# Adding b2 - beta1 on GpSimd instead of by a product with ones, in a four-layer graph kernel on one core

## The chip, the cores and the metric

The kernel runs on one core of one Trainium2 chip. The metric is the device time of one execution in microseconds (us), lower is better. In the profile PE is TensorE (PEld its weight loads), DVE is VectorE, ACT is ScalarE, POOL is GpSimd and SP the engine that issues most of the DMAs.

## What is computed

The input is x, 64 graphs of 256 nodes with 256 features, and adj, a 256 x 256 adjacency matrix for each. Four layers follow each other, each x = layernorm(x + layer(x, adj)) over the features. All is float32.

```python
# layer 0: 4 heads of 64
attn = softmax(where(adj == 0, -1e9, q @ k.T / 8));  out = (attn @ v) @ Wo.T + bo;  out = norm(out) * gamma + beta
# layer 1: 8 heads of 32, one projection for q, k and v, then an MLP
n = norm(x) * gamma1 + beta1
x = x + attention(n, n, n, adj)
y = norm(x) * gamma2 + beta2
out = x + gelu(y @ W1 + b1) @ W2 + b2
# layer 2: graph attention, leaky_relu(s1 + s2) as scores;  layer 3: edge scores by adj == 1..4
```

## The kernel before, in words

`usual_input` does the work; `any_input` is a slower second way that is taken when a flag says that the values are unusual, and is not taken here. A group is two graphs, so 512 rows in four blocks of 128; there are 32 groups. `group(g)` is a generator: each `yield` ends a *turn*, and a group has 45 turns. Several groups are in work at the same time, each in another stage, and the row `ORDER` says in which order their turns are written into the program: in period p the digit a stands for the next turn of group p - a. `FIRST` and `LAST` do the same for the ramps. `prepare`, the setup that the first groups do not need at once, is one more generator and takes its turns beside group 0.

The order of PE is exactly the order in which its instructions are written: `matmul` and `transpose` chain them. On the other engines a scheduler places the instructions of all groups in the queue, so an instruction of a later turn can stand ahead of one of an earlier turn.

The turns of a group that the text speaks of (L numbers are lines of the kernel before):

| turns | what they do |
|---|---|
| 1 to 3 | loads of x and adj; adj to bfloat16 (adjb, L889) and its square sum (L890) on ACT; four transposing DMAs to adjT (L897) |
| 4 | mask on DVE (L900, adjT and adjb); transposes of x on PE, copies on ACT (L584) |
| 5 to 7 | q, k and v projections; then x + beta0 on POOL (L717), which waits for the transposes of x |
| 8 to 10 | layer 0: scores, exp on ACT (L605), times mask on DVE (L607), products with v and with ones; reciprocal of the sums (L641) |
| 11 to 13 | sums over DRAM to all rows (lines, rr); oT times rr on DVE (L732); product with Wo |
| 14, 15 | two norms on DVE with the power of the variance on POOL (L547, L551); the results are z (L559) and xb (L750) |
| 17 | transposes of z on PE, to zT (L586, ACT) |
| 18 to 22 | layer 1: four times scores of 16 matmuls on 32 rows, exp (L605), times mask on DVE with sums (L613, 8 for each), products with z |
| 21, 23, 24 | in `behind`: transposes back, x2 = y / sums + xb (L770, L773), `both` = x2 + xb on POOL (L774), norm to xb (L559) |
| 26 to 30 | transposes of xb, W1 and gelu on ACT (L788) |
| 31 to 34 | W2, a graph in two turns of 8 float32 products each, 16 records of the profile |
| 33, 35 | y = W2 product + `both` on DVE (L699), norm to xn |
| 36 to 40 | layer 2 |
| 41 to 45 | layer 3; the result goes out by DMA |

The second product of the MLP needs x2 + xb - beta1 + b2 added, since xb carries beta1. Before the change POOL makes x2 + xb, and b2 - beta1 comes in on PE: `b2m` holds it in three rows of bfloat16, whose sum is the float32 value nearly to the last bit, and `onesb` has ones in three rows and zeros elsewhere. A product of the two, 128 x 128 by 128 x 512 in bfloat16, opens each accumulation (`row` in `project`). In PSUM there are two score tiles (`ps`, two banks each) and four tiles of one bank (`pm`).

Of the kernel before, what the change touches and what calls it, by code (L numbers as in the profile page):

```python
# [8 lines left out]
F32 = mybir.dt.float32  # L9
BF16 = mybir.dt.bfloat16  # L10
# [3 lines left out]
ALU = mybir.AluOpType  # L14
AX = mybir.AxisListType

P = 128
N = 256
D = 256
NC = D // P  # L20
G = 2
QB = N // P
# [11 lines left out]
AT_ONCE = 3  # L34


ORDER = "011225334342343542234235432323132121321132121"


FIRST = "0010000201000100213100110101000000100"  # L40
# [360 lines left out]
def usual_input(ctx: ExitStack, tc: tile.TileContext, a: dict, out: bass.AP, flag: bass.AP):  # L401
# [7 lines left out]
    nc = tc.nc  # L409
    B = a["x"].shape[0]  # L410

    const = ctx.enter_context(tc.tile_pool(name="const", bufs=1))
# [44 lines left out]
    def load_rows(name, cols, queue=None):  # L457

        src = a[name]
        t = const.tile([P, src.shape[0] // P, cols], F32, name=name)  # L460
        load(queue, t, src.rearrange("(c p) f -> p c f", p=P))
        return t
# [7 lines left out]
    setup = act.tile([P, NF, T], F32, name="setup", tag="hT", bufs=1).rearrange("p f t -> p (f t)")  # L470

    def load_all(src, name, at=None):

        t = const.tile([P, D], F32, name=name) if at is None else setup[:, at:at + D]
        load(None, t, src.unsqueeze(0).to_broadcast([P, D]))
        return t
# [18 lines left out]
    beta1r = load_all(a["L1_gnn_beta1"], "beta1r")  # L495
    gamma1r = load_all(a["L1_gnn_gamma1"], "gamma1r", 256)
    b2 = load_all(a["L1_gnn_b2"], "b2", 512)
# [7 lines left out]
    w2 = load_rows("L1_gnn_W2", D)  # L505

    wa1 = const.tile([P, 2, NC], F32, name="wa1")
    b2m = const.tile([P, D], BF16, name="b2m")
    onesb = const.tile([P, P], BF16, name="onesb")
    bop = const.tile([P, D], F32, name="bop")  # L510
    bounds = const.tile([P, 2], F32, name="bounds")

# [1 line left out]
    def over_blocks(v, n=TB):  # L514
        return v.unsqueeze(1).to_broadcast([P, n, D])
# [3 lines left out]
    def in_order(ins):  # L519

        if on_pe:
            tc.add_manual_dep(ins.ins, on_pe.pop(),
                              mybir.DependencyInfo(mybir.DependencyClass.NoSync, mybir.DependencyReason.DATA),
                              reason="the order of the program")
        on_pe.append(ins.ins.name)

    def matmul(*args, **kw):
        in_order(nc.tensor.matmul(*args, **kw))  # L528

    def transpose(*args):  # L530
        in_order(nc.tensor.transpose(*args))  # L531

    def blocks(i):
        return range(i * QB, (i + 1) * QB)
# [22 lines left out]
    def scaled(dst, src, i, mv, rstd):  # L557
        for q, t in enumerate(blocks(i)):
            nc.vector.tensor_scalar(dst[:, t, 0:D], src[:, t, 0:D], mv[:, q, 0:1], rstd[:, q:q + 1],  # L559
                                    ALU.subtract, ALU.mult)  # L560

    ALL = range(G)
# [114 lines left out]
            go_on()  # L677
            yield

    def project(dst, srcT, w, extra, row=None, gs=ALL):  # L680


        chunks = w.shape[1]
        for i in gs:
            pm = ps_m.tile([P, QB, D], F32, name="pm")
            if row is not None:
                matmul(pm, onesb, row.unsqueeze(1).to_broadcast([P, QB, D]), start=True, stop=False)
            for q in range(QB):
                t = i * QB + q
                for c in range(chunks):  # L690
                    matmul(pm[:, q, :], srcT[:, c, t * P:(t + 1) * P], w[:, c, :],
                           start=c == 0 and row is None, stop=c == chunks - 1 and (row is None or q == QB - 1))
                if chunks > NC:
                    yield
            o = dst[:, i * QB:(i + 1) * QB, :]
            if extra is None:
                nc.scalar.copy(o, pm)
            else:
                nc.vector.tensor_tensor(o, pm, extra[:, i * QB:(i + 1) * QB, 0:D], ALU.add)  # L699
# [56 lines left out]
    def layer1(xb, z, mask):  # L756

        zT = transposed(z, gamma1, beta1)
        x2 = act.tile([P, TB, D], F32, name="y")
        both = act.tile([P, TB, W], F32, name="both", tag="xn")  # L760
        yield

        def behind(i, oT, r):
            nc.vector.reciprocal(r, r)
            pt = ps_m.tile([P, QB, D], F32, name="pm")
            for q in range(QB):
                for c in range(NC):
                    transpose(pt[:, q, c * P:(c + 1) * P], oT[:, c, q * P:(q + 1) * P], ident)
            o = x2[:, i * QB:(i + 1) * QB, :]
            nc.vector.tensor_tensor(o.rearrange("p q (h d) -> p (q h) d", d=32), pt.rearrange("p q (h d) -> p (q h) d", d=32),  # L770
                                    r.rearrange("p q c h -> p (q c h)").unsqueeze(2).to_broadcast([P, QB * 8, 32]), ALU.mult)
            xi = xb[:, i * QB:(i + 1) * QB, :]
            nc.vector.tensor_tensor(o, o, xi, ALU.add)  # L773
            nc.gpsimd.tensor_tensor(both[:, i * QB:(i + 1) * QB, 0:D], o, xi, ALU.add)  # L774
            yield
            mv, rstd = stats(x2, i)
            scaled(xb, x2, i, mv, rstd[:, 0])
            yield

        yield from attention(zT, zT, z, mask, 32, gamma1, behind)  # L780
        yT = transposed(xb, gamma2, beta2)
        yield
        hT = act.tile([P, NF, T], F32, name="hT", bufs=1)
        for f in range(NF):
            pm = ps_m.tile([P, T], F32, name="pm")
            for c in range(NC):
                matmul(pm, w1[:, c, f * P:(f + 1) * P], yT[:, c, :], start=c == 0, stop=c == NC - 1)
            nc.scalar.activation(hT[:, f, :], pm, AF.Gelu, bias=b1[:, f:f + 1])  # L788
            if f % 2:
                yield  # L790
        return x2, hT, both
# [93 lines left out]
    def group(g):  # L885
        x, adj = load_group(g) if g else first
        yield
        adjb = io.tile([P, TB, N], BF16, name="adjb", bufs=1)
        nc.scalar.activation(adjb, adj, AF.Copy, accum_out=there[:, g:g + 1])  # L889
        nc.scalar.activation(adj.bitcast(F32), adj, AF.Square, bias=minus_half, accum_out=edges[:, g:g + 1])  # L890
        yield


        pt = io.tile([P, G, QB, N], BF16, name="adjT", bufs=1)
        for t in range(TB):
            i, q = divmod(t, QB)
            nc.sync.dma_start_transpose(pt[:, i, :, q * P:(q + 1) * P], adjb[:, t, :])  # L897
        yield
        mask = act.tile([P, G, QB * N], BF16, name="mask")
        nc.vector.scalar_tensor_tensor(mask.rearrange("p g k -> p (g k)"), pt.rearrange("p g k q -> p (g k q)"), 1.0,  # L900
                                       adjb.rearrange("p t k -> p (t k)"), ALU.mult, ALU.min,
                                       accum_out=both_ways[:, g:g + 1])
        xb, z = yield from layer0(g, x, mask)
        y, hT, both = yield from layer1(xb, z, mask)

        def others(gs):

            yield from project(y, hT, w2, both, b2m, gs)
            x = yield from renormed(y, gs)
            x = yield from layer2(x, mask, gs)  # L910
            x = yield from layer3(g, x, mask, gs)
            i, j = g * G + gs[0], g * G + gs[-1] + 1
            nc.sync.dma_start(out[i:j].rearrange("b (q p) d -> p (b q) d", p=P), x[:, gs[0] * QB:(gs[-1] + 1) * QB, 0:D])

        if g < B // G - 1:
            yield from others(ALL)
            return

        parts = [others((i,)) for i in ALL]
        turn = 0  # L920
        while parts:
            for r in parts[:turn // QB + 1]:
                if next(r, END) == END:
                    parts.remove(r)
            turn += 1
            yield

    def prepare():
# [8 lines left out]
        pm = ps_m.tile([P, D], F32, name="pm")  # L937
# [12 lines left out]

        yield

        nc.gpsimd.memset(onesb, 0.0)
        nc.gpsimd.memset(onesb[0:3, :], 1.0)
        nc.gpsimd.memset(b2m, 0.0)
        left = setup[:, 2304:2560]
        nc.vector.tensor_tensor(left, b2, beta1r, ALU.subtract)
        for k in range(3):
            part = setup[:, 3328 + k * P:3456 + k * P].bitcast(BF16)
            nc.vector.tensor_copy(part, left)  # L960
            nc.sync.dma_start(b2m[k:k + 1, :], part[0:1, :])
            if k < 2:
                nc.vector.tensor_tensor(left, left, part, ALU.subtract)

        yield

        sq = setup[:, 2816:3328].rearrange("p (s d) -> p s d", s=2)
        nc.vector.tensor_tensor(sq[:, 0], gamma1r, gamma1r, ALU.mult)
# [8 lines left out]
        pm = ps_m.tile([P, 2], F32, name="pm")  # L977
# [26 lines left out]
    for period in range(len(groups)):  # L1004
        for age in ORDER:
            g = period - int(age)
# [22 lines left out]
    pm = ps_m.tile([P, 1], F32, name="pm")  # L1029
# [38 lines left out]
```

## The time and the profile before

| | us |
|---|---|
| median of the three runs shown | 2663.03 |
| lowest, highest | 2661.43, 2664.4 |
| span of the profiled execution | 2658.2 |
| PE busy | 2586.9 (97%) |
| DVE, ACT, POOL busy | 1965.7, 1293.9, 592.3 |
| b2m products on PE (64) | 24.6 in all by their own length, 384 ns each |
| adds of `both` on POOL (64) | 81.4, 1272 ns each |
| adds of beta0 on POOL (32) | 77.7, 2430 ns each |

The profiled execution has no time of its own beside its span; the median of the runs is 4.8 us above that span, for what lies before the first and after the last instruction. In a group of instructions of the profile, "busy" counts overlapping lengths once; matmuls are pipelined, so what one costs PE is read from its start to the start of the next.

### The profile page before, as it was taken

Reading aid. Unit: us, or ns where it says so; the run is one execution under the profiler, and the core shown is the slowest. Engines: PE = TensorE matmul, PEld = TensorE weight load, DVE = VectorE, ACT = ScalarE, POOL = GpSimd, SP = SyncE. Lnnn points to the kernel's source line nnn. Section 1 sums busy time; section 2 is a strip of 40 time slices with the busy share of each in tenths; the row PEclk is TensorE's granted clock in tenths of the full one; section 3 lists DMA queues with packets and bytes.
Section 4 is the critical chain, followed back from the end, with each engine's and each line's share of the span. In section 5 each row is a group of like instructions: output and inputs, shape, how many; then the busy total and the mean of one; then the engine's idle time right before and its main releaser. Section 6 shows DMA issues by size and latency. Waiting matters only on the chain.

```text
span 2658.2 us, 44921 instructions
## 1 busy us (share of the span) xinstructions
PE 2586.9 (97%) x16648; PEld 1761.5 (66%) x16648; DVE 1965.7 (74%) x6189; ACT 1293.9 (49%) x1997; POOL 592.3 (22%) x1145
## 2 busy tenths in 40 slices
PE   6899999999999999999999999999999999999996
PEld 3567667666667666666676666676676676676665
DVE  4667777777777777777777777777777777777774
ACT  3445544545545545545455544555445455445442
POOL 2112222222222222222222222222222222222121
PEclk8999999999999999999999999999999999999998
DMA  6001011001010000010010110110110101000000
GB/s 163 25 9 32 26 37 37 25 29 29 29 37 29 33 29 28 29 37 27 28 36 25 33 37 25 29 37 21 36 37 25 29 29 29 29 21 17 17 1 25
DMA packets 113393, 83.20 MB, mean 31 GB/s; under 512 B 44304, under 2 KB 112656, under 8 KB 113168
## 3 DMA queue, kind: packets, MB, share of 16 engines
q1 hardware_dynamic: 111552, 78.94, 10.1%
q8 instruction: 134, 2.20, 0.4%
q10 hardware_dynamic: 1360, 0.79, 0.1%
q0 software_dynamic: 256, 0.53, 0.1%
q14 instruction: 91, 0.75, 0.1%
HBM read 54.80 MB, written 17.04 MB: 27 GB/s over the span
## 4 chain that ended last, share of the span: by engine, by line
PE 71%; DVE 17%; POOL 9%; issue 2%; DMA 1%; ACT 0%; SPq 0%; DVEq 0%; POOLq 0%; ACTq 0%
PE pm L528 55%; PE ps L528 10%; PE pm L531 7%; POOL rstd L551 6%; DVE st L544 3%; DVE y L816 2%; DVE y L744 2%; DVE xn L559 2%; POOL ve L547 2%; DVE z L559 2%; DVE mv L545 1%; DVE xb L750 1%; DVE y L743 1%; DVE r L815 1%; POOL ve L549 0%
## 5 line engine op out<-in xcount | busy, mean ns | idle before, releaser
L613 DVE SCALAR_TENSOR_TENSOR e<-e,mask 128x256 f32<-128x256 f32 x1024 | 428.2, 483 | 130.7 <-ACT e L605 130.7
L605 ACT ACTIVATE e<-ps 128x1024 f32<-128x1024 f32 x384 | 371.9, 1020 | 196.2 <-PE ps L528 176.3
L528 PE MATMUL pm<-L_gnn_W,hT 128*128 128x256 f32 x2048 | 463.0, 379 | 0.0
L528 PE MATMUL pm<-xT,L_gnn_W 128*128 128x512 f32 x1024 | 455.2, 592 | 0.0
L528 PEld LDWEIGHTS pm<-L_gnn_W,hT 128*128 128x128 f32 x2048 | 384.5, 190 | 49.2 <-issue 0.7
L788 ACT ACTIVATE hT<-pm,b 128x512 f32<-128x512 f32 x256 | 176.7, 691 | 408.1 <-PE pm L528 408.0
L528 PEld LDWEIGHTS pm<-xT,L_gnn_W 128*128 128x128 f32 x1024 | 191.7, 190 | 203.4 <-issue 198.5
L544 DVE BATCH_NORM_STATS2 st<-y 128x6 f32<-128x256 f32 x768 | 301.1, 408 | 6.7
L551 POOL TENSOR_TENSOR rstd<-ve,mhalf 128x2 f32<-128x2 f32 (+1 forms) x384 | 298.4, 777 | 26.7
L559 DVE TENSOR_SCALAR xn<-y,mv,rstd 128x256 f32<-128x256 f32 x384 | 141.9, 411 | 178.9 <-POOL rstd L551 178.8
L547 POOL TENSOR_SCALAR ve<-mv 128x2 f32<-128x2 f32 x384 | 98.9, 257 | 741.0 <-DVE mv L545 738.8
L774 POOL TENSOR_TENSOR both<-y,xb 128x512 f32<-128x512 f32 x64 | 81.4, 1272 | 764.2 <-DVE y L773 764.2
L607 DVE TENSOR_TENSOR e<-e,mask 128x1024 f32<-128x1024 f32 x128 | 150.8, 1221 | 15.3 <-ACT e L605 15.3
L528 PE MATMUL ps<-xT 32*128 32x256 f32 x2048 | 148.0, 402 | 2.2 <-ACT e L605 1.3
L586 ACT ACTIVATE xT<-pm,beta,gamma 128x512 f32<-128x512 f32 x128 | 92.3, 770 | 104.4 <-PE pm L531 104.3
L528 PE MATMUL pm<-e,z 128*32 128x256 f32 x2048 | 142.4, 387 | 0.3
L528 PEld LDWEIGHTS ps<-xT 32*128 32x128 f32 x2048 | 93.2, 185 | 74.0 <-issue 66.8
L528 PE MATMUL pm<-e,v 128*32 128x256 f32 x2048 | 125.4, 384 | 8.0 <-DVE e L607 8.0
L528 PE MATMUL pm<-L_gnn_WoT,oT 128*128 128x256 f32 x512 | 121.2, 391 | 8.3 <-DVE oT L732 6.0
L528 PE MATMUL ps<-qT,kT 64*128 64x256 f32 x1024 | 128.0, 389 | 0.5 <-ACT e L605 0.5
L528 PE MATMUL pm<-xT,L_gnn_WqT 128*128 128x512 f32 x256 | 120.9, 616 | 3.7 <-ACT xT L584 3.7
L816 DVE SCALAR_TENSOR_TENSOR y<-pm,r,xn 128x256 f32<-128x256 f32 x256 | 120.9, 473 | 2.5
(138 smaller groups left out, 4059.1 us busy)
## 6 DMA issues: line engine op xcount, KB each, us to landing
x<-in_x SPq DMA_DIRECT2D x32, 512.0 KB
adj<-in_adj SPq DMA_DIRECT2D x32, 512.0 KB
rr<-lines SPq DMA_DIRECT2D x124, 128.0 KB
out<-xn SPq DMA_DIRECT2D x31, 512.0 KB
adjT<-adjb SPq DMA_TRANSPOSE x128
L_gnn_W<-in_L_gnn_W SPq DMA_DIRECT2D x2, 1024.0 KB
lines<-zs SPq DMA_DIRECT2D x62, 4.0 KB
rr<-lines POOLq DMA_DIRECT2D x4, 128.0 KB, 3.3
```

What stands on the lines that cost most here:

```text
L528: in_order(nc.tensor.matmul(*args, **kw))
L531: in_order(nc.tensor.transpose(*args))
L544: nc.vector.bn_stats(st[:, q, :], src[:, t, 0:D])
L547: nc.gpsimd.tensor_scalar(ve[:, 0], mv[:, :, 1], EPS, None, ALU.add)
L551: nc.gpsimd.tensor_tensor(rstd, ve, mhalf[:, 0:k * QB].rearrange("p (k t) -> p k t", k=k), ALU.pow)
L559: nc.vector.tensor_scalar(dst[:, t, 0:D], src[:, t, 0:D], mv[:, q, 0:1], rstd[:, q:q + 1], ALU.subtract, ALU.mult)
L586: nc.scalar.activation(dst[:, c, on], pt[:, on], AF.Identity, bias=bias[:, c:c + 1], scale=scale[:, c:c + 1])
L605: nc.scalar.activation(e, ps, AF.Exp, scale=scale)
L607: nc.vector.tensor_tensor(e, e, mask.unsqueeze(1).to_broadcast([P, 2, QB * N]), ALU.mult)
L613: nc.vector.scalar_tensor_tensor(e[:, h, k], e[:, h, k], 1.0, mask[:, k], ALU.mult, ALU.mult, accum_out=sums[:, kc, c, j:j + 1])
L788: nc.scalar.activation(hT[:, f, :], pm, AF.Gelu, bias=b1[:, f:f + 1])
L816: nc.vector.scalar_tensor_tensor(y[:, t, :], po[:, 0:D], r, x[:, t, 0:D], ALU.mult, ALU.add)
```

## The change

Two things change. First, b2m becomes a float32 tile with b2 - beta1 in all 128 rows, made by one subtraction in `prepare`; the three bfloat16 parts, their three DMAs, `onesb`, three memsets and one turn of `prepare` go. `project` loses the product that opened the accumulation, and a second POOL operation in `behind`, written after the norm to xb, adds b2m to `both`. Second, ORDER is another row with the same number of digits of each kind.

```diff
-ORDER = "011225334342343542234235432323132121321132121"
+ORDER = "510324231342354343452223431232321232111321213"
...
-    b2m = const.tile([P, D], BF16, name="b2m")
-    onesb = const.tile([P, P], BF16, name="onesb")
+    b2m = const.tile([P, D], F32, name="b2m")
...
-    def project(dst, srcT, w, extra, row=None, gs=ALL):
+    def project(dst, srcT, w, extra, gs=ALL):
...
-            if row is not None:
-                matmul(pm, onesb, row.unsqueeze(1).to_broadcast([P, QB, D]), start=True, stop=False)
...
                     matmul(pm[:, q, :], srcT[:, c, t * P:(t + 1) * P], w[:, c, :],
-                           start=c == 0 and row is None, stop=c == chunks - 1 and (row is None or q == QB - 1))
+                           start=c == 0, stop=c == chunks - 1)
...
             xi = xb[:, i * QB:(i + 1) * QB, :]
+            bi = both[:, i * QB:(i + 1) * QB, 0:D]
             nc.vector.tensor_tensor(o, o, xi, ALU.add)
-            nc.gpsimd.tensor_tensor(both[:, i * QB:(i + 1) * QB, 0:D], o, xi, ALU.add)
+            nc.gpsimd.tensor_tensor(bi, o, xi, ALU.add)
             yield
             mv, rstd = stats(x2, i)
             scaled(xb, x2, i, mv, rstd[:, 0])
+            nc.gpsimd.tensor_tensor(bi, bi, over_blocks(b2m, QB), ALU.add)
             yield
...
-            yield from project(y, hT, w2, both, b2m, gs)
+            yield from project(y, hT, w2, both, gs)
...
-        nc.gpsimd.memset(onesb, 0.0)
-        nc.gpsimd.memset(onesb[0:3, :], 1.0)
-        nc.gpsimd.memset(b2m, 0.0)
-        left = setup[:, 2304:2560]
-        nc.vector.tensor_tensor(left, b2, beta1r, ALU.subtract)
-        for k in range(3):
-            part = setup[:, 3328 + k * P:3456 + k * P].bitcast(BF16)
-            nc.vector.tensor_copy(part, left)
-            nc.sync.dma_start(b2m[k:k + 1, :], part[0:1, :])
-            if k < 2:
-                nc.vector.tensor_tensor(left, left, part, ALU.subtract)
-
-        yield
+        nc.vector.tensor_tensor(b2m, b2, beta1r, ALU.subtract)
```

With the turns of the table, the two rows read as follows from the place where the first W2 turn (31) stands; the number in brackets is the age of the group.

```
before: 31(3) 17(2) 32(3) 18(2) 33(3)  4(1) 34(3) 19(2)  5(1) 20(2)  6(1) 35(3) 21(2)  7(1)  8(1) 36(3) 22(2)  9(1) 23(2) 10(1)
after:  31(3)  4(1) 17(2) 32(3) 18(2) 33(3) 19(2)  5(1) 20(2) 34(3) 21(2)  6(1)  7(1)  8(1) 35(3) 22(2)  9(1) 23(2) 10(1) 36(3)
```

## The prediction

> **What bounds the kernel now.** I read the page's head first: which engine is full, and which chain ended last.
>
> ```profile
> span 2658.2 us, 44921 instructions
> PE 2586.9 (97%) x16648; PEld 1761.5 (66%) x16648; DVE 1965.7 (74%) x6189; ACT 1293.9 (49%) x1997; POOL 592.3 (22%) x1145
> PE 71%; DVE 17%; POOL 9%; issue 2%; DMA 1%; ACT 0%; SPq 0%; DVEq 0%; POOLq 0%; ACTq 0%
> ```
>
> TensorE (PE) is the bound, and its order is written by hand. So a product that is taken away pays in full, and any late input of PE costs in full. The add of beta0 (POOL L717) starts at 1023.43 and again at 1103.90, 1184.23: one period of ORDER is 80.33 us. Here is PE in the part that the new row rearranges (columns: start, duration, engine, line, operation; idle before in brackets).
>
> ```profile
> 1089.14 0.38 PE L528 MATMUL pm<-b2m,onesb 128*128 128x512 bf16 x1
> 1089.35 3.62 PE L528 MATMUL pm<-L_gnn_W,hT 128*128 128x256 f32 x16
> 1092.81 0.38 PE L531 MATMUL pm<-ident,z 128*128 128x128 f32 x2
> 1093.48 1.16 PE L531 MATMUL pm<-ident,z 128*128 128x128 f32 x6 [0.29 <-DVE z L559]
> 1094.48 3.62 PE L528 MATMUL pm<-L_gnn_W,hT 128*128 128x256 f32 x16
> 1098.03 1.15 PE L528 MATMUL ps<-xT 32*128 32x256 f32 x16
> 1099.11 0.39 PE L528 MATMUL pm<-b2m,onesb 128*128 128x512 bf16 x1
> 1099.33 3.62 PE L528 MATMUL pm<-L_gnn_W,hT 128*128 128x256 f32 x16
> 1102.79 1.04 PE L531 MATMUL pm<-ident,x 128*128 128x128 f32 x8
> 1103.66 3.62 PE L528 MATMUL pm<-L_gnn_W,hT 128*128 128x256 f32 x16
> 1107.21 1.15 PE L528 MATMUL ps<-xT 32*128 32x256 f32 x16
> ```
>
> Read start to start, since matmuls are pipelined. The bias product takes 0.21 us (1089.14 to 1089.35). The eight transposes of z take 1.67 us (1092.81 to 1094.48) where the same eight of x take 0.87 (1102.79 to 1103.66): PE loses 0.80 us there, waiting for VectorE's z. The first scores of layer 1 (1098.03) come 9.18 us before the second (1107.21). From 1000 to 2400 us the list of PE's waits has this one line (total, times, longest; it counts less than start to start, as ends are modelled):
>
> ```profile
> PE pm L531 <- DVE z L559: 5.3, 18, 0.3
> ```
>
> Then the other engines in the same stretch, from their timelines:
>
> ```profile
> 1093.74 0.88 DVE L750 SCALAR_TENSOR_TENSOR xb<-z,rstd,beta1r 128x256 f32<-128x256 f32 x2
> 1096.58 1.23 DVE L900 SCALAR_TENSOR_TENSOR mask<-adjT,adjb 128x1024 bf16<-128x1024 bf16 x1
> 1104.04 2.57 DVE L613 SCALAR_TENSOR_TENSOR e<-e,mask 128x256 f32<-128x256 f32 x1
> ```
> ```profile
> 1103.90 2.43 POOL L717 TENSOR_TENSOR x<-x,beta 128x1024 f32<-128x1024 f32 x1 [2.97 <-PE pm L531]
> ```
> ```profile
> 1097.84 1.06 ACT L889 ACTIVATE adjb<-adj 128x1024 bf16<-128x1024 int32 x1 [2.15 <-DVE mask L900]
> 1100.17 1.92 ACT L605 ACTIVATE e<-ps 128x1024 f32<-128x1024 f32 x2
> ```
>
> Two things are to be seen. An L613 takes 0.42 us, but the one under GpSimd's L717 takes 2.57: 2.15 us longer. The steady periods all show it. And ScalarE's queue holds the exponentials of layer 1 (L605) behind adjb (L889), which waits for VectorE's mask (L900).
>
> [...] bn_stats under GpSimd's L774 keep their length (0.75 us for two at 1125.13, 0.75 at 1098.86 without). [...]
>
> **The change, part by part.** I use the trace's durations and the order of the two built programs, on this period's clock.
>
> 1. *Bias product gone.* 64 x 0.21 = 13.4 us of PE, all on the path: 0.43 per period with two, and 6 outside the 29 steady periods with the new pattern, 1.3 us.
>
> 2. *GpSimd add.* 64 x 1.27 us (L774's duration; same shape, b2m read by broadcast) is 81 us; POOL goes from 592 to about 674 us, 25%. It stands right behind L774, ahead of the variance step L547 of the same half. In the first half that delays rstd and xb by up to 1.27, and behind xb stand layer 0's mask products (L607), for which PE waits. Today these end at 1130.47 for a PE start at 1130.62: 0.15 spare. The new row puts the k projection (3.63) between the transposes of oT and these products and takes the xn transposes (1.02) out: 2.6 us more room. So 0.15 + 2.6 - 1.27 leaves about 1.4, and I cost it at nothing; without that cover, 1.27 per period. In the second half the variance step already waits for VectorE (1.80 idle): nothing. VectorE works there on bn_stats, reciprocals and tensor_scalars, with one SBUF input. I take no collision; the bound is 1.27 x 64 = 81 us of VectorE, which has 26% idle.
>
> 3. *Setup.* Five VectorE operations, three memsets and three DMAs go, and one turn of prepare. The DMAs hold SP from 25.15 to 28.49, ahead of four transposing DMAs; the mask behind them starts at 37.31, and PE waits 6.86 us to 39.73. Gain 0 to 3.3; I take 2.
>
> 4. *The row.* In old terms PE runs: W2 half, z transposes, W2, first scores, W2, x transposes, W2, second scores. New: W2, **x transposes**, z transposes, W2, first scores, W2, **second scores** and their product; the last W2 turn comes after two more. SP's DMAs (out, x, adjacency transposes, adj, lines, rr) keep their cyclic order, and POOL issues DMAs for group 0 alone. The closest is rr: VectorE's oT product (L732) already waits 0.45 us for it at 1061.12, with PE not held; I cost it at nothing, up to 0.5 per period.
>
>  - *z:* x's 0.87 stands before z, less 0.21 of bias. z transposes start at 1089.14 + 3.46 + 0.87 = 1093.47 and reach the second half of z after it is ready. The 0.80 goes.
>  - *xn* transposes leave the gap between 64-row and 32-column products: start to start 1.02 there, 0.87 elsewhere. I take 0.1.
>  - *L717 moves onto VectorE's chain.* It starts 1.11 after the x transposes start (1102.79 to 1103.90): now 1092.60 + 1.11 = 1093.71, to 1096.14. At 1093.74 VectorE enters L750, then L873, L875, L900: all with two SBUF inputs, back to back. They lose the 2.15 of the profile. The mask ends at 1097.81 + 2.15 = 1099.96; adjb starts at 1099.99, and L605, 2.33 later as today, at 1102.32; its two tiles end at 1103.29 and 1104.24.
>  - *What is late next:* the second scores stand at 1093.47 + 0.88 + 3.55 + 1.08 + 3.46 = 1102.44, 1.07 long, their product from 1103.51 to 1104.51. The score tiles are two, and both hold the first scores until L605 has read them: the second pair of heads starts at about 1104.34, and both rows of keys end at 1105.2. The product needs eight L613 at 0.346 (start to start) from 1103.37: the seventh at 1105.79, the last at 1106.14. With 0.43 for each of its last two steps and 0.1 for the switch, the q projection starts at 1106.8 instead of 1104.51: **2.3 us lost per period**. Bounds 1.9 to 2.8. Without the collision L605 ends at 1102.09, as today, and the loss is 0.1.
>
> Sum per period: -0.43 - 0.80 - 0.10 + 2.3 = +0.97, so a period of 81.3. Times 29: +28; less 2 and 1.3: about **+25**. Against the span of the profiled execution, 2658.2, that is 2683; the median of the runs shown is 2663.03, 4.8 above the span, so 2688.
>
> **The rivals.**
>  - *A, faster:* the collision is not there or falls in a gap, and the second scores wait 0.1. Period -0.43 - 0.80 - 0.10 + 0.1 = -1.23, times 29 is -36, less 3.3: 2624, and up to 2655 with smaller new stalls. For it: PE is 97% busy and its work shrinks. Against it: L717 and L750 would start 0.03 us apart, and VectorE stays in two-input work for 4 us. It decides at a mask delay of about 1.2 us, where the loss equals the gain of 1.33.
>  - *B, slower still:* the two adds in a row make xb and L607 late after all, 1.27 per period: 25 + 37, 2725. Against it: the 1.4 us of room.
>  - *C, no change:* half the loss, 2658 to 2668; or the bias goes but the row is eaten up elsewhere.
>
> **How the numbers follow.** 0.2% (5.3 us) is about what a measurement can tell from no change. Forecast 0.68, its own range 2672 to 2712 (the bounds of the loss, and waits such as rr's); A 0.15; B 0.12; C 0.05. Slower 0.80, same 0.05, faster 0.15. For eight in ten the range reaches down into A and nearly to B: 2640 to 2722.
>
> **What would show it.** Right: one VectorE operation per period, L750 or its neighbour, of about 2.6 us instead of 0.45; ScalarE waiting for the mask 4.3 us instead of 2.15; PE idle before second scores and their product about 2 us per period, released by ACT e and DVE e; z's wait gone; no bf16 matmul; starts of the beta0 add 81.3 apart. Wrong: the starts at 79.2 and no long L750 (A), or PE waiting for L607 with xb held by GpSimd (B).

## The result, and the profile after

| | before | after |
|---|---|---|
| median of the runs (four of each) | 2662.3 us | 2702.32 us (2699.02 to 2704.2) |
| ratio | | 1.0149, 95% interval 1.0135 to 1.0164 |
| span of the profiled execution | 2658.2 | 2697.3 |
| one regular period | 80.33 | 81.52 |

The change makes the kernel 1.5% slower, 40 us. The page after, in the three lines that were shown of before:

```profile
span 2697.3 us, 44755 instructions
PE 2606.6 (97%) x16584; PEld 1765.3 (65%) x16584; DVE 2012.4 (75%) x6184; ACT 1293.4 (48%) x1997; POOL 668.3 (25%) x1206
PE 60%; DVE 23%; POOL 9%; ACT 5%; issue 3%; DMA 1%; SPq 0%; POOLq 0%; DVEq 0%; ACTq 0%
```

PE issues 64 matmuls fewer and is busy 20 us longer. Matmul records overlap (below, the transposes of x end at 1109.12 and those of z start at 1108.95), and one is some 0.4 us long (382 ns for those of W2), so a short wait shows in part only: of the 0.80 us that z cost before, 0.29 was idle. The busy row can't tell work from short waits. The chain can: PE's share falls from 71% to 60%, and VectorE's and ScalarE's rise from 17% and 0% to 23% and 5%. PE's timeline in the part that the row rearranges (start, duration, engine, line, operation):

```profile
1108.08 1.04 PE L530 MATMUL pm<-ident,x 128*128 128x128 f32 x8
1108.95 1.15 PE L530 MATMUL pm<-ident,z 128*128 128x128 f32 x8
1109.94 3.62 PE L527 MATMUL pm<-L_gnn_W,hT 128*128 128x256 f32 x16
1113.49 1.15 PE L527 MATMUL ps<-xT 32*128 32x256 f32 x16
1114.56 3.72 PE L527 MATMUL pm<-L_gnn_W,hT 128*128 128x256 f32 x16
1118.79 0.70 PE L527 MATMUL ps<-xT 32*128 32x256 f32 x4 [0.50 <-ACT e L604]
1119.70 1.13 PE L527 MATMUL ps<-xT 32*128 32x256 f32 x12 [0.21 <-ACT e L604]
1120.76 1.61 PE L527 MATMUL pm<-e,z 128*32 128x256 f32 x16
1122.31 3.70 PE L527 MATMUL pm<-xT,L_gnn_WqT 128*128 128x512 f32 x8
```

The wait for z is gone: the eight transposes of z take 0.99 us instead of 1.67. In its place the second scores (1118.79) stop twice for ScalarE's exponentials, and their product lasts 1.61 instead of the 1.07 of an undisturbed one. The other engines in the same stretch, each from its timeline:

```profile
1109.20 2.69 POOL L714 TENSOR_TENSOR x<-x,beta 128x1024 f32<-128x1024 f32 x1 [0.83 <-PE pm L530]
```
```profile
1109.20 2.98 DVE L747 SCALAR_TENSOR_TENSOR xb<-z,rstd,beta1r 128x256 f32<-128x256 f32 x2
1114.14 1.22 DVE L899 SCALAR_TENSOR_TENSOR mask<-adjT,adjb 128x1024 bf16<-128x1024 bf16 x1
```
```profile
1115.40 1.06 ACT L888 ACTIVATE adjb<-adj 128x1024 bf16<-128x1024 int32 x1 [4.20 <-DVE mask L899]
1117.73 1.92 ACT L604 ACTIVATE e<-ps 128x1024 f32<-128x1024 f32 x2
```

(L747, L899, L888 and L604 after are L750, L900, L889 and L605 before.) The beta0 add and xb start at the same instant. The two xb operations take 2.98 us, where before they took 0.88; the mask and adjb are late by as much, and behind adjb stand the exponentials. Over 1000 to 2400 us the list of waits has two lines for this chain (total, times, longest):

```profile
ACT adjb L888 <- DVE mask L899: 71.4, 17, 4.2
PE ps L527 <- ACT e L604: 12.3, 34, 0.5
```

Each regular period has one such wait of adjb, 4.2 us, and two of PE.

### The profile page after: what moved, and what is told of

Same layout as the page of the kernel before. It is cut to its first block, busy times and chain, and to the rows that moved or that the text cites. A ratio compares the mean times of both kernels' runs of the same rounds, so it can differ in the third digit from the quotient of the medians.

```text
span 2697.3 us, 44755 instructions
## 1 busy us (share of the span) xinstructions
PE 2606.6 (97%) x16584; PEld 1765.3 (65%) x16584; DVE 2012.4 (75%) x6184; ACT 1293.4 (48%) x1997; POOL 668.3 (25%) x1206
## 4 chain that ended last, share of the span: by engine, by line
PE 60%; DVE 23%; POOL 9%; ACT 5%; issue 3%; DMA 1%; SPq 0%; POOLq 0%; DVEq 0%; ACTq 0%
PE pm L527 47%; PE ps L527 8%; POOL rstd L550 6%; PE pm L530 4%; DVE xb L747 4%; DVE st L543 3%; DVE y L815 2%; ACT e L604 2%; DVE y L741 2%; DVE xn L558 2%; POOL ve L546 2%; DVE z L558 1%; DVE mask L899 1%; DVE mv L544 1%; ACT adj L889 1%
## 5 line engine op out<-in xcount | busy, mean ns | idle before, releaser
L612 DVE SCALAR_TENSOR_TENSOR e<-e,mask 128x256 f32<-128x256 f32 x1024 | 364.2, 422 | 177.0 <-ACT e L604 177.0
L527 PE MATMUL pm<-L_gnn_W,hT 128*128 128x256 f32 x2048 | 469.2, 382 | 0.0
L604 ACT ACTIVATE e<-ps 128x1024 f32<-128x1024 f32 x384 | 371.9, 1020 | 197.4 <-issue 104.3
L527 PEld LDWEIGHTS pm<-L_gnn_W,hT 128*128 128x128 f32 x2048 | 379.1, 190 | 69.9 <-issue 23.5
L546 POOL TENSOR_SCALAR ve<-mv 128x2 f32<-128x2 f32 x384 | 88.7, 231 | 1245.0 <-DVE mv L544 1243.5
L558 DVE TENSOR_SCALAR xn<-y,mv,rstd 128x256 f32<-128x256 f32 x384 | 190.7, 543 | 118.6 <-POOL rstd L550 118.5
L527 PE MATMUL ps<-xT 32*128 32x256 f32 x2048 | 167.0, 404 | 22.4 <-ACT e L604 21.5
L527 PEld LDWEIGHTS ps<-xT 32*128 32x128 f32 x2048 | 100.7, 184 | 95.4 <-ACT e L604 45.6
L527 PE MATMUL pm<-e,z 128*32 128x256 f32 x2048 | 158.4, 388 | 0.6
L527 PE MATMUL pm<-xn,qT 128*128 128x257 f32 x512 | 120.0, 388 | 3.1
```

The lines of the kernel that those rows point to most:

```text
L546: nc.gpsimd.tensor_scalar(ve[:, 0], mv[:, :, 1], EPS, None, ALU.add)
L604: nc.scalar.activation(e, ps, AF.Exp, scale=scale)
L612: nc.vector.scalar_tensor_tensor(e[:, h, k], e[:, h, k], 1.0, mask[:, k], ALU.mult, ALU.mult, accum_out=sums[:, kc, c, j:j + 1])
```

## The experiments

Three theories were set against each other. **Theory 1**, the forecast's: the beta0 add collides with VectorE's two-input chain, mask and adjb are late, and adjb holds the exponentials. **Theory 2**: the new row puts second scores and product too close to the first, collision or not. **Theory 3**: the second add of GpSimd is what costs. Where time is given by pairs of PE's operations, it is summed from the start of one matmul to the start of the next over 18 regular periods, and divided by 18. Each ratio is to the kernel before as it ran beside that kernel (medians of 2660.6 to 2662.1 us), so for small differences the ratios say more than the times.

| kernel | us | ratio to before, interval | period |
|---|---|---|---|
| after without beta0 add | 2643.56 | 0.9933 (0.9917 to 0.9950) | 79.50 |
| after, two buffers for adjb | 2701.1 | 1.0148 (1.0131 to 1.0165) | 81.52 |
| before + new row | 2695.87 | 1.0129 (1.0112 to 1.0146) | 81.52 |
| after with old row | 2676.19 | 1.0055 (1.0038 to 1.0072) | 80.59 |
| after, adjb behind exponentials | 2772.53 | 1.0419 (1.0402 to 1.0437) | 84.02 |
| after, beta0 add held | 2643.58 | 0.9937 (0.9921 to 0.9954) | 79.50 |
| before + new row, beta0 add held | 2646.02 | 0.9944 (0.9927 to 0.9961) | 79.74 |
| after without second add | 2695.56 | 1.0130 (1.0113 to 1.0147) | 81.54 |
| before, beta0 add held | 2681.27 | 1.0071 (1.0054 to 1.0087) | 80.96 |
| after, both adds late | 2639.96 | 0.9917 (0.9901 to 0.9934) | 79.50 |
| the last, xn earlier | 2683.27 | 1.0080 (1.0063 to 1.0097) | 80.92 |

### Without the beta0 add

```diff
-        nc.gpsimd.tensor_tensor(x, x, over_blocks(beta0), ALU.add)
```

> The changed kernel without the beta0 add on GpSimd (it leaves out beta0, which is zero in these inputs). Theory 1: no operation of VectorE of about 3 us in the chain before the mask, mask 2.1 us earlier, the 2.3 us of a period become 0.1 to 0.3: a period of about 79.3 to 79.5, the whole 2632 to 2645. Theory 2 (the row is too close even without the collision): 2695 to 2702. Theory 3 (the second add): 2695 to 2702, up to the little that GpSimd gains.

2643.56 us, a period of 79.50. VectorE's pair of xb operations is short again:

```profile
1087.31 0.87 DVE L746 SCALAR_TENSOR_TENSOR xb<-z,rstd,beta1r 128x256 f32<-128x256 f32 x2
```

In after 28 of them are stretched, in this kernel none. 28 times the 2.02 us that come back in a period make 57; the medians of the two kernels lie 59 apart, the spans of their profiled executions 54. So the period explains nearly all of it, and theories 2 and 3 fall as main causes. How the add reaches PE isn't shown by this alone.

### Two buffers for adjb

```diff
-        adjb = io.tile([P, TB, N], BF16, name="adjb", bufs=1)
+        adjb = io.tile([P, TB, N], BF16, name="adjb", bufs=2)
```

> The changed kernel with two buffers for adjb instead of one. adjb of one group then need not wait for the mask of the group before, so it no longer stands in ScalarE's queue with the exponentials behind it; the mask itself is still made late. Theory 1 (the beta0 add collides with VectorE's chain, mask late, adjb late, exponentials late): the wait of adjb for the mask, 135 us between 1000 and 2400 us, falls under 20; most of the 2.3 us of a period comes back, leaving at most 0.5; a period of about 79.6 instead of 81.5, the whole about 2640 to 2650 against 2702. VectorE's long operation under the beta0 add stays. Theory 2 (the new row places second scores and their product too close to the first, collision or not): 2695 to 2702. Theory 3 (the second add of GpSimd is what costs, by way of VectorE): 2695 to 2702.

2701.1 us, no change, and adjb's wait for the mask is still 71.4 us in 17 times from 1000 to 2400 us, as in after (the 135 of the expectation is the sum over the whole run). By itself that would speak for theory 2. But the order of ScalarE's queue tells otherwise: with a second buffer the scheduler takes adjb forward by one group, until it waits for the same mask in the same place. The edit did not take the wait away, so this run decides nothing.

### The new row alone

```diff
-ORDER = "011225334342343542234235432323132121321132121"
+ORDER = "510324231342354343452223431232321232111321213"
```

> The kernel before with the new row alone: b2 - beta1 still by the bfloat16 product, no second add on GpSimd, the old set-up. Theory 1: the loss is the row's, so the whole is the changed kernel plus the bias products, 64 times 0.21 = 13 us, less what the second add may cost: 2705 to 2718. Theory 3 (the second add costs, the row is free or a gain): about 2635 to 2663. The start, with the DMAs of the old set-up, tells whether the 2.4 us that the changed kernel is late in its first regular period are the row's or the set-up's.

2695.87 us: the row alone makes nearly the whole loss, as theory 1 says, but 9 to 22 us less than expected. The period is 81.52, exactly that of after, though this kernel still has both bias products. Between the two, by pairs: the product is 0.44 us in this kernel; after has 0.24 more before the second scores, 0.11 more among the W2 matmuls and 0.09 more among the transposes of z. The sum is zero. So while the mask is late, taking the product out of the regular periods brings nothing.

### The old row with the add

```diff
-ORDER = "510324231342354343452223431232321232111321213"
+ORDER = "011225334342343542234235432323132121321132121"
```

> The changed kernel with the old row: the add on GpSimd alone. The second product of a period with z was held by z anyway, so of 0.43 of a period about 0.21 can be gained there, 6 us, and 1 to 3 at the ends. If the add of the first half is free: 2652 to 2658. If it makes xb and layer 0's mask products late, as the 0.15 us of room in the old row says it should (1.27 - 0.15 = 1.1 us a period): 2685 to 2695, with PE waiting before the products of layer 0's last scores. Theory 3 expects the loss of the changed kernel here too, about 2700.

2676.19 us, between the expectations, and slower than before by 15. Per period the product gives 0.44; 0.21 goes back to the wait for z, which VectorE sets, 0.11 to the W2 matmuls, and 0.39 to layer 0's products with v, which now wait for mask products (0.27 + 0.12). The mechanism of the expectation is there, at a third of its size: 0.39 instead of 1.1.

### adjb behind the exponentials

```diff
-                nc.scalar.activation(e, ps, AF.Exp, scale=scale)
+                exps.append(nc.scalar.activation(e, ps, AF.Exp, scale=scale).ins.name)
...
-        nc.scalar.activation(adjb, adj, AF.Copy, accum_out=there[:, g:g + 1])
+        cast = nc.scalar.activation(adjb, adj, AF.Copy, accum_out=there[:, g:g + 1])
+        if exps:
+            tc.add_manual_dep(cast.ins, exps[-1],
+                              mybir.DependencyInfo(mybir.DependencyClass.NoSync, mybir.DependencyReason.DATA),
+                              reason="behind the exponentials")
```

Both operations are ScalarE's, and in its timeline adjb (1094.31) now stands right behind a pair of exponentials (1092.48, 1.94 us).

> The changed kernel, with the conversion adjb of a group ordered on ScalarE behind the exponentials of layer 0 (a second buffer had not moved the wait: the scheduler used it to take adjb of a later group forward to the same place). The collision stays: VectorE's L747 of about 3 us and the mask late by 2.1. Theory 1: only adjb carried the late mask to the exponentials, so these start when their scores are there, and second scores and product lose at most 0.5 of a period: about 79.5 to 80.0 instead of 81.52, 2643 to 2660. Theory 2 (VectorE's chain itself, not ScalarE's queue, is what second scores wait for): 81.0 to 81.5, 2690 to 2702.

2772.53 us, far off the expectation. But the trace settles the link that was asked for. VectorE's and PE's timelines:

```profile
1142.01 2.98 DVE L748 SCALAR_TENSOR_TENSOR xb<-z,rstd,beta1r 128x256 f32<-128x256 f32 x2
```
```profile
1147.38 3.72 PE L528 MATMUL pm<-L_gnn_W,hT 128*128 128x256 f32 x16
1151.03 1.15 PE L528 MATMUL ps<-xT 32*128 32x256 f32 x16
1152.10 1.19 PE L528 MATMUL pm<-e,z 128*32 128x256 f32 x16
```

The collision is there (2.98), and the second scores run in one piece with no wait; from the middle W2 turn to the q projection it is 10.47 us (1142.75 to 1153.22) against 12.37 after (1109.94 to 1122.31). The mask is as late as in after (6.17 us from the start of xb to its end in both), and with the exponentials ahead of adjb PE loses 0.12 us there, in the product. The longer period, 84.02, comes from elsewhere, as two lines of its waits say:

```profile
DVE oT L730 <- DMA rr<-lines: 53.7, 14, 4.8
PE pm L531 <- DVE y L816: 39.8, 17, 3.4
```

VectorE's oT product waits for rr, and behind it stands an operation that PE waits for. SP's timeline shows why rr is late. The edit put adjb behind the last exponential written before it, and that moved adjb by some 30 us (37.2 us behind the transposes of x, where after has 7.3). Its transposing DMAs now fill SP's queue right ahead of those of `lines` and `rr`:

```profile
1095.48 5.08 SPq L901 DMA_TRANSPOSE adjT<-adjb  x4
1100.66 0.52 SPq L446 DMA_DIRECT2D adj<-in_adj  x1
1101.28 0.57 SPq L726 DMA_DIRECT2D lines<-zs  x1
1104.88 1.25 SPq L728 DMA_DIRECT2D rr<-lines  x2
```

Counted from the transposes of x, the DMA to `lines` is issued 1.6 us later than in after, and the first to `rr` 3.5 us later. So the order of SP's queue, which the change leaves alone and the prediction priced at nothing, costs some 4 us a period where it is disturbed (an estimate: 84.02, less the 0.12, against the 79.50 of the kernel without the beta0 add).

### The beta0 add held behind y

```diff
-                nc.vector.tensor_tensor(o, pm, extra[:, i * QB:(i + 1) * QB, 0:D], ALU.add)
+                evac.append(nc.vector.tensor_tensor(o, pm, extra[:, i * QB:(i + 1) * QB, 0:D], ALU.add).ins.name)
...
-        nc.gpsimd.tensor_tensor(x, x, over_blocks(beta0), ALU.add)
+        add = nc.gpsimd.tensor_tensor(x, x, over_blocks(beta0), ALU.add)
+        if evac:
+            tc.add_manual_dep(add.ins, evac[-1],
+                              mybir.DependencyInfo(mybir.DependencyClass.Sync, mybir.DependencyReason.DATA),
+                              reason="behind y")
```

GpSimd's add now waits for VectorE's y, which stands right behind the mask.

> The changed kernel, with the beta0 add of GpSimd held until VectorE has taken y out of the second product of the MLP, which VectorE does just behind the mask. Nothing is left out; only the collision is moved off the chain before the mask, on to an evacuation from PSUM and bn_stats. Theory 1: as without the beta0 add, period 79.4 to 79.7, 2640 to 2652. If GpSimd's queue behind the add (the variance step of y) or the products of mask and exponentials then lie under it, up to 0.5 of a period more, 2665. Theory 2 (row too close in itself): 2690 and more.

2643.58 us: nothing is left out, and the kernel is 0.6% faster than before. VectorE and PE in its timelines:

```profile
1086.45 0.87 DVE L752 SCALAR_TENSOR_TENSOR xb<-z,rstd,beta1r 128x256 f32<-128x256 f32 x2
1089.28 1.23 DVE L904 SCALAR_TENSOR_TENSOR mask<-adjT,adjb 128x1024 bf16<-128x1024 bf16 x1
```
```profile
1095.46 1.15 PE L528 MATMUL ps<-xT 32*128 32x256 f32 x16
1096.54 1.07 PE L528 MATMUL pm<-e,z 128*32 128x256 f32 x16
```

xb is back at 0.87, adjb waits 2.1 us for the mask, and second scores and product run without a gap. By pairs, after loses 2.02 us a period to this kernel, all in one place: 0.58 before the second scores, 0.90 within them and 0.55 in the product.

### The same with the bias product

To the kernel before, the two edits of the new row and of the held beta0 add (L numbers move by a few):

```diff
-ORDER = "011225334342343542234235432323132121321132121"
+ORDER = "510324231342354343452223431232321232111321213"
...
-        nc.gpsimd.tensor_tensor(x, x, over_blocks(beta0), ALU.add)
+        add = nc.gpsimd.tensor_tensor(x, x, over_blocks(beta0), ALU.add)
+        if evac:
...
```

> As the kernel with the late beta0 add, but with b2 - beta1 by the bfloat16 product as before and no second add: the kernel before with the new row and the beta0 add held. Against that kernel it tells what the exchange of product for add is worth where PE is not held by the late mask. By the forecast's prices the product is 0.43 of a period, so this one should be 12 to 14 us slower than it. With the old row the exchange cost 15 us instead of gaining; if VectorE and GpSimd lose as much to the second add here, this one is 5 to 15 us faster.

2646.02 us. With the late mask out of the way the exchange of product for add is worth 0.25 us a period (79.74 to 79.50): 0.44 of product, less 0.11 among the W2 matmuls and 0.09 at z. The place of layer 0's products with v is unchanged, so in the new row there is room for the add, as forecast. Of 29 x 0.25 = 7 us only 2.4 are left between the medians (4.0 between the spans of the profiled executions); the rest must be lost in the ramps.

### Without the second add

```diff
-            nc.gpsimd.tensor_tensor(bi, bi, over_blocks(b2m, QB), ALU.add)
```

> The changed kernel without the second add of GpSimd (it leaves out b2 - beta1). The row-only kernel and the changed one have the same period, 81.52, although the product was taken out. If the second add costs what the product gained (0.43): a period of 81.1, about 2690. If the late mask alone sets the period, by a loop in which neither product nor add stands: 81.52 again, about 2700. If the second add is the main cause (theory 3): 2660 or less.

2695.56 us, with a period of 81.54: the late mask sets it. The second add costs 5 to 7 us in all (5.2 between the spans of the profiled executions, 5 by the two ratios, 6.8 between the medians), none of it in regular periods. It costs where a group is alone, first of all group 0, as PE's timelines show, first of after, then of this kernel:

```profile
110.51 1.65 PE L530 MATMUL pm<-ident,xb 128*128 128x128 f32 x6 [6.72 <-DVE xb L558]
```
```profile
107.38 1.65 PE L530 MATMUL pm<-ident,xb 128*128 128x128 f32 x6 [5.38 <-DVE xb L558]
```

For each half PE waits 1.34 us longer for xb (6.72 against 5.38, and 1.80 against 0.45), about one GpSimd add of 1.27: it stands ahead of the variance step, and no other group's work covers it. At the other end, with the last group, it is the same once more:

```profile
2614.95 1.09 PE L530 MATMUL pm<-ident,xb 128*128 128x128 f32 x6 [2.39 <-DVE xb L558]
```
```profile
2609.34 1.09 PE L530 MATMUL pm<-ident,xb 128*128 128x128 f32 x6 [1.06 <-DVE xb L558]
```

The three make 4.0 us. The groups of VectorE's xn in the page (busy, mean ns of one), of after and of this kernel, show a second thing:

```profile
L558 DVE TENSOR_SCALAR xn<-y,mv,rstd 128x256 f32<-128x256 f32 x384 | 190.7, 543 | 118.6 <-POOL rstd L550 118.5
```
```profile
L558 DVE TENSOR_SCALAR xn<-y,mv,rstd 128x256 f32<-128x256 f32 x384 | 160.8, 465 | 118.5 <-POOL rstd L550 118.4
```

In after, 60 of the 384 take over 0.6 us; without the second add, 30; in the kernel before, 1. A tensor_scalar with one SBUF tensor, 0.41 us alone, was held beside these GpSimd adds: one under the first add of `both`, one under the second, 1.17 and 1.39 us in the period at 1138. The row decides whether they meet: the new row alone, without a second add, has 30 of them, and the old row with the second add has 2. The 30 of the second add cost PE nothing in the regular periods: with and without them the period is the same.

### The kernel before with the beta0 add held

```diff
-        nc.gpsimd.tensor_tensor(x, x, over_blocks(beta0), ALU.add)
+        add = nc.gpsimd.tensor_tensor(x, x, over_blocks(beta0), ALU.add)
+        if evac:
...
```

> The kernel before with the beta0 add held behind VectorE's y, and nothing else: old row, bias product. It completes a square of row by place of the beta0 add (old and early 2661, new and early 2696, new and late 2646). Theory 1: in the old row the collision lies on a product of mask and exponential that PE doesn't wait for, so moving it brings nothing, 2655 to 2665; the beta0 add decides only with the new row. If holding the add alone brought the gain: 2635 to 2650.

2681.27 us, against an expected 2655 to 2665: holding the add is no gain in itself, but it isn't neutral either. GpSimd's and VectorE's timelines:

```profile
1443.12 2.36 POOL L718 TENSOR_TENSOR x<-x,beta 128x1024 f32<-128x1024 f32 x1 [7.15 <-DVE y L700]
1445.44 0.22 POOL L548 TENSOR_SCALAR ve<-mv 128x2 f32<-128x2 f32 x1
1445.75 0.71 POOL L552 TENSOR_TENSOR rstd<-ve,mhalf 128x2 f32<-128x2 f32 x1
```
```profile
1446.50 0.73 DVE L560 TENSOR_SCALAR xn<-y,mv,rstd 128x256 f32<-128x256 f32 x2 [2.46 <-POOL rstd L552]
1447.15 0.42 DVE L614 SCALAR_TENSOR_TENSOR e<-e,mask 128x256 f32<-128x256 f32 x1
```

The held add stands in GpSimd's queue ahead of y's variance step (1445.44). So rstd is late, VectorE waits 2.46 us with xn, and layer 1's products of mask and exponentials, which stand behind xn in VectorE's queue, start at 1447.15. PE's products with z grow by 0.66 us a period, and nothing else changes by more than 0.03. The move pays only with the new row: neither the row alone (1.0129) nor the held add alone (1.0071) makes the kernel faster, both together do (0.9944).

### Both adds late

```diff
-            nc.gpsimd.tensor_tensor(bi, bi, over_blocks(b2m, QB), ALU.add)
...
-            nc.scalar.activation(hT[:, f, :], pm, AF.Gelu, bias=b1[:, f:f + 1])
+            gelu = nc.scalar.activation(hT[:, f, :], pm, AF.Gelu, bias=b1[:, f:f + 1])
+            if f == 0:
+                ball = both[:, :, 0:D]
+                add = nc.gpsimd.tensor_tensor(ball, ball, over_blocks(b2m), ALU.add)
+                tc.add_manual_dep(add.ins, gelu.ins.name,
+                                  mybir.DependencyInfo(mybir.DependencyClass.Sync, mybir.DependencyReason.DATA),
+                                  reason="behind the first gelu")
```

This and the held beta0 add are the two edits to the kernel after.

> The changed kernel with the beta0 add held, and b2 - beta1 added to both halves at once, behind the first gelu of the group, instead of half by half ahead of the variance step. It tells where the second add costs. In the ramp PE waits for the first group's xb 1.35 and 1.34 us longer than without the second add, and these 2.7 us should come back; in the regular periods nothing of it shows on PE, so the period stays at 79.5, or falls by up to 0.1 with the residual wait for z. The whole 2637 to 2642 against 2643.6. If VectorE's stretched xn (30 of 60 slow ones come from the second add) held PE somewhere, more: 2630.

2639.96 us, the fastest of all: 0.83% below before and 62 below after. Group 0's waits for xb are back at 0.45 and 5.38, the period stays at 79.50. Against the kernel with the beta0 add alone held, the span of the profiled execution is 2.8 us shorter, as expected, the median 3.6. Only 30 xn are stretched, and PE gains nothing from that.

### The transposes of xn earlier

```diff
-ORDER = "510324231342354343452223431232321232111321213"
+ORDER = "510324231342354343452223431232321232111321231"
```

The row ends with 9(1) 23(2) 36(3) 10(1), instead of 9(1) 23(2) 10(1) 36(3).

> As the kernel with both adds late, and in the row the transposes of xn (turn 36) ahead of layer 0's last step (turn 10) instead of behind it. All kernels with the new row lose 0.26 and 0.08 us a period between the transposes of qT and layer 3's product, because the transposes of xn stand right ahead of them and their banks are still being copied. If that is the reason, 0.34 of a period comes back: 79.15, and 10 us of the whole, 2627 to 2632. If the pm banks are then short elsewhere (oT, the values of layer 0), as much is lost again: no gain or slower.

2683.27 us: slower by 43. The wait in question does go: from the transposes of qT to layer 3's product it is 0.28 us instead of 0.49. But the transposes of xn take 0.35 us longer at their new place, and within the product PE loses 1.26 us more, for which its list of waits names the reason:

```profile
PE pm L528 <- ACT pm L642: 18.1, 17, 1.1
```

The product needs the bank in which layer 0's sums still stand until VectorE's reciprocal and ScalarE's L642 have read them. Ahead of it the xn transposes had given that bank time. So, as this reads, the four one-bank tiles are the limit there, and the small wait was the cheaper of the two; a kernel with more such tiles was not tried.

## Why the prediction was right, and where its sizes were off

**Direction and mechanism: right.** Put on the clock of the trace after (the forecast's times plus 15.48, by the start of the first W2 turn), the chain came as worked out:

| | forecast | measured |
|---|---|---|
| beta0 add starts | 1109.19 | 1109.20 |
| mask ends | 1115.44 | 1115.37 |
| adjb starts | 1115.47 | 1115.40 |
| exponentials start | 1117.80 | 1117.73 |
| q projection starts | 1122.28 | 1122.31 |

Each link was shown apart: the beta0 add by leaving it out and by moving it, and adjb by ordering it behind the exponentials. Rival A, the same change without the collision, was priced at 2624 to 2655, and the kernel with the add held takes 2643.58.

**Sizes: 39.1 us of span instead of 25.** The period was +1.19 instead of +0.97 (6.4 us in 29), and the rest +4.6 instead of -3.3. By the steps of the sum:

1. *Bias product, -0.43.* Mis-sized: the exchange of product for add is worth 0.25 where PE is free to use it, and nothing beside the late mask. Start to start the product takes 0.44, but 0.11 comes back among the W2 matmuls once it no longer stands between the scores and them, and 0.09 at z.
2. *GpSimd add at nothing.* Right in the regular periods of the new row. It failed in the ramps, which the step didn't look at: 5 to 7 us. Rival B had the mechanism, two adds ahead of xb, but not the place: it acts where no other group covers it, and by 0.39 a period in the old row. "I take no collision" was wrong on VectorE: tensor_scalars were held under GpSimd's adds (1.17 and 1.39 us instead of 0.41), and the summed length of xn rises from 157.9 to 208.6 us. Half of that, to 178.6, comes with the new row alone, and the second add's half costs PE nothing in the regular periods. Of these operations with one SBUF input the forecast had measured bn_stats alone, and it took the tensor_scalars to be like them. bn_stats, 0.38 to 0.43 us each, were not held: two take 0.75 us under the held beta0 add, as without one. Why the one is held and the other not was not shown.
3. *Setup, -2.* It brought nothing there. SP issues the four transposing DMAs at 26.98 instead of 28.58, but they keep the queue 7.64 us instead of 5.96, and the mask starts at 38.58 instead of 37.31. All the kernels here agree: with the old set-up the four keep the queue 5.6 to 6.0 us, with the new one 7.0 to 7.9. That SP was held ahead of them was true; that the transfers would land earlier was not. The mask's start differs by some 2 us between kernels of one set-up, and how the DMAs share the time stays open.
4. *z, -0.80.* Measured -0.77 (before against the new row with the beta0 add held).
5. *xn, -0.10.* About -0.15 at their old place. But the step missed what stands next to their new place: transposes of qT and layer 3's product, which need banks that are still being copied. That costs 0.35 us a period (0.28 + 0.07) in the kernels with the new row but the last, and is the largest missing term. Moving the transposes, in the last kernel, took the small wait away and brought a larger one.
6. *Late chain, +2.3.* Measured +2.02 against the kernel with the add held. The end of the chain was right to 0.03 us; the undisturbed chain, from which the loss was counted, takes 15.68 us from W2 to the q projection (1081.86 to 1097.54) and not 15.37, by items such as the 0.11 and 0.09 above.

The five measured terms, -0.25 - 0.77 - 0.15 + 0.35 + 2.02, make +1.20 against 1.19. That the forecast's period came so near is in part luck: the late chain was taken 0.28 us too large, and that hid about half of the 0.51 by which the other terms were too favourable. Outside the regular periods the forecast missed 7.9 us (+4.6 instead of -3.3). The second add's 5 to 7 in the ramps and the set-up's 2 are about that much; single runs of after differ by 5 us (2699.02 to 2704.2), so nothing can be read from what is left.

## What to carry to other kernels

When a row of turns is rearranged, follow not only the bound engine: ask which GpSimd operation now starts beside which VectorE chain, and what stands in another engine's queue behind the chain's last result, as the exponentials stood behind adjb's wait of 4.2 us. The same collision of GpSimd with VectorE cost PE nothing where VectorE's queue had slack (before, 2.15 us on VectorE), and more than a whole period's gain where the end of the stretched chain released the next step (after, 2.02 us a period); holding one add back by 5.2 us (from 1.1 to 6.3 us behind the start of the transposes of x) turned 1.5% slower into 0.6% faster. And work taken off the bound engine pays only from where that engine isn't waiting: the same product was worth 0, or 0.25, or a loss, by row and by the place of the add that replaced it.

## What the runs showed of the hardware that was not expected

- A float32 tensor_scalar of VectorE, one SBUF tensor of 128 x 256 and two scalars per partition, 0.41 us alone, took 1.17 and 1.39 us beside GpSimd adds of 1.27. In the new row each of the two adds stretches one of them per group, about 30 in a kernel.
- GpSimd's add was longer in the collision too, the more so the more of VectorE's operation was left when it started. Where it meets bn_stats the beta0 add takes 2.36 us. In the kernel before, with the new row alone and in after it starts while an operation with two SBUF inputs has 0.21, 0.27 and 0.48 us to run, and takes 2.42, 2.49 and 2.70, less that rest 2.21, 2.22 and 2.22. VectorE's next operation was then held: in the kernel before and in after it takes 2.57 and 2.58, and ends 0.28 us behind the add.
- Which of the two was held went with hundredths of a microsecond. In the kernel without the second add, the add and the first xb operation start within 0.03 us of each other. In 13 of 28 periods GpSimd is ahead by 0.012 to 0.025 us: its add takes 2.36, and the first xb operation 2.62. In the other 15 it is ahead by at most 0.015: the add takes 2.70, the first xb operation 0.48 and the second 2.58. The pair of xb takes 3.0 us either way, so the period hardly shows which came first (81.52 to 81.59 us). One period of each kind, by GpSimd and VectorE:

```profile
1024.34 2.35 POOL L714 TENSOR_TENSOR x<-x,beta 128x1024 f32<-128x1024 f32 x1 [0.81 <-PE pm L530]
1187.45 2.70 POOL L714 TENSOR_TENSOR x<-x,beta 128x1024 f32<-128x1024 f32 x1 [0.82 <-PE pm L530]
```
```profile
1024.36 3.01 DVE L747 SCALAR_TENSOR_TENSOR xb<-z,rstd,beta1r 128x256 f32<-128x256 f32 x2
1187.45 2.98 DVE L747 SCALAR_TENSOR_TENSOR xb<-z,rstd,beta1r 128x256 f32<-128x256 f32 x2
```

- A bfloat16 product between scores on 32 rows (32*128) and float32 matmuls on 128 rows (128*128) cost less than its own start to start: of the 0.23 us of the second of a period, 0.11 appears among the W2 matmuls behind it when it is taken out. Why was not tried.
- Four transposing DMAs that were issued 1.6 us earlier (26.98 instead of 28.58) kept SP's queue 1.7 us longer (7.64 instead of 5.96), and so it was in all nine kernels with the new set-up against the four with the old. Why was not tried.
